# Reordered side tasks, a direct division and a split last projection in a two-layer attention kernel

## The chip, the cores and the metric

The kernel runs on one core of one Trainium2 chip, in one launch. The metric is the time of the device in microseconds. Before the change it was run three times: 3338.06, 3339.32 and 3341.99 us, median 3339.32. One execution more was profiled. Engines are named as in the profile: PE is TensorE (PEld its weight loads), ACT ScalarE, DVE VectorE, POOL GpSimd, SP the engine that issues most transfers.

## The reference

The input x has 4 images of 256 channels and 64 x 64 pixels, in float32. Two attention layers follow each other, each behind a group norm of 32 groups and with a residual:

```
x = x + L0(_gn(x))        # layer 0
x = x + L1(_gn(x))        # layer 1

L0: q = Wq x;  k, v = 2x2 convolutions of x with stride 2 (1024 positions)
    attn = softmax((q·k + q·(rel_h + rel_w)) * 32**-0.5) per head, 8 heads of 32
    out = v attn
L1: q, k, v = 1x1 convolutions (w_qkv, b_qkv)
    the 4096 pixels are cut into 4 areas of 1024; softmax attention within each area
    out = out + depthwise 7x7 convolution of v (w_pe, b_pe)
    out = 1x1 convolution (w_proj, b_proj)
```

The softmax is computed without subtracting the maximum; the kernel sums divisors and reciprocals into `sums` and checks at the end that none is out of bounds, for which a second path stands ready.

## The kernel before

**Units and steps.** The attention of both layers is cut into 128 units: 8 blocks (`BLOCKS`: layer 0, written A, of images 0 to 3, then layer 1, written B, of images 0 to 3) of 16 units. A unit is one half of the channels (4 heads) of one chunk of 512 queries against 1024 keys, and has 8 steps of 128 keys. So the main loop has 1024 steps. In step j TensorE computes four score matmuls into two PSUM pairs (`scores`, L262), ScalarE exponentiates each pair (`exps`, L266), TensorE multiplies the probabilities of the step before with v (`weighted`, L273), and VectorE adds the probabilities to those of step 0 (`sum_up`, L795: two additions of 128x1024 per step, except for the first step of a unit). When a unit's eight steps are done, its `av` is copied out (L816), and three steps after its last step, which is step 2 of the next unit, the summed probabilities are multiplied with ones (`divisors`, L282).

**Division.** `divide` (L291 to L312) copies the divisors, sends one row per head through DRAM to 128 partitions of 16 numbers, takes the reciprocals there (step 7 of the next unit), sends them back and spreads them, and multiplies in step 4 of the unit after that. The four transfers are issued by GpSimd. Only the last unit takes the reciprocal of the whole 128x512 tile on VectorE (L294) and multiplies at once; its divisors and reciprocals are kept in `spare` and summed later by `sum_last`, two reductions.

**Side tasks.** All other work (projections for q, k and v, the depthwise convolution as matmuls, the output projection) is cut into tasks of one to four parts. `plan` is a dictionary from (unit, step) to functions, filled by `plan_a`, `plan_b`, `plan_values` and `plan_conv`; `at(g, j, f)` enters one. A function either issues something at once (a transfer on SP, a normalization on ScalarE, statistics on VectorE) or appends a task to the queue `side`. After a step's attention the loop executes one part if the queue isn't empty, a second one if more than 7 parts wait and a third one if more than 14 wait, one less in step 2, and all of them of one task. `soon_tasks` inserts tasks directly behind the head instead of appending them. `need(made, key)` executes parts at once until what an attention step needs exists: q and k when a step's scores are issued, v when its first weighted product is issued (that is in step 1 of a unit, behind the scores of that step). `plan_conv` uses it too, for the last values. Every task's result goes into one PSUM tile, `side`, with one buffer, and is copied out by ScalarE or VectorE at the end of the task.

**Tasks by layer.** For layer 0 of image b, `plan_a` loads the image's chunks for the statistics (`look`, `add_stats`) from unit `early`, forms the norm, and for each of four areas loads two chunks, normalizes eight `taps` on ScalarE and appends two k and two v tasks. `prep` is the first unit of the block before. Queries (`make_q`) are appended two units ahead of their use. For layer 1, `plan_b` appends k, v and q tasks; `plan_values` computes the values that the convolution reads, `plan_conv` is the convolution (units 70.5 to 106), and after it come the projections (`add_conv` adds convolution, bias and attention, `project` multiplies and adds the residual): those of images 0 to 2 are spread over units 108 to 125, those of image 3 follow their own attention. All chunks share one tag with six buffers, the taps one with three, and the probabilities one with ten.

**The end.** The last chunk's projection starts when unit 127's attention has been multiplied: VectorE adds both halves of the channels, TensorE multiplies two tasks, VectorE adds bias and residual, and one transfer writes 512 KB. Then `sums` is compared with its limit, the count goes to a register, and the program ends.

The loop around all this:

```
ps[j], exps = scores(units[g], j)
exps[0]()
for f in later.pop(now[0], []): f()      # sums, divisors, divide
if before is not None: weighted(*before)
exps[1]()
do(g, j)                                  # the plan's functions
# then one to three parts of the queue's head
```

Of the kernel before, what the change touches and what calls it, by code (L numbers as in the profile page):

```python
# [12 lines left out]
ALU = mybir.AluOpType  # L13
AX = mybir.AxisListType

P = 128
# [38 lines left out]
def direct_path(  # L55
# [149 lines left out]
    def plan_norm(key, g, j):  # L205

        name = f"{key[0]}{key[1]}"
        made = {}

        def aggregate():  # L210
            for tag, cols in (("mv", 2), ("gmean", 1), ("dev", 1), ("gvar", 1)):
                shape = [P, CT, cols] if cols > 1 else [P, CT]
                made[tag] = pool.tile(shape, FP, tag=tag, name=f"{tag}_{name}", bufs=2)
            mv = made["mv"]
            for t in range(CT):
                V.bn_aggr(out=mv[:, t, :], in_=stats[key][:, t].rearrange("p c s -> p (c s)"))

        def means():
            mv, mean, dev = made["mv"], made["gmean"], made["dev"]
            ps = ps_pair(f"gm_{name}")[:, 0, :CT]  # L220
            T.matmul(ps, lhsT=gmat, rhs=mv[:, :, 0], start=True, stop=True)
            S.copy(mean, ps)
            V.tensor_sub(dev, mv[:, :, 0], mean)
            V.tensor_mul(dev, dev, dev)
            V.tensor_add(dev, dev, mv[:, :, 1])

        def variances():
            ps = ps_pair(f"gv_{name}")[:, 0, :CT]
            T.matmul(ps, lhsT=gmat, rhs=made["dev"], start=True, stop=True)
            S.activation(made["gvar"], ps, AF.Identity, bias=eps)  # L230
            norm = pool.tile([P, 2, CT], FP, tag="norm", name=f"norm_{name}", bufs=8)
            shift, rstd = norm[:, 0, :], norm[:, 1, :]
            G.tensor_tensor(rstd, made["gvar"], neghalf, ALU.pow)
            G.tensor_tensor(shift, made["gmean"], rstd, ALU.mult)
            G.tensor_scalar(shift, shift, -1.0, None, ALU.mult)
            norms[key] = shift, rstd

        at(g, j, aggregate)
        at(g, j + 1, means)
        at(g, j + 3, variances)  # L240

    def normalize(key, dst, src, t):
        shift, rstd = norms[key]
# [34 lines left out]
    def divisors(g, p):  # L278

        dens[g] = ps_pair("den")[:, 0, :]  # L280
        for h in range(4):
            T.matmul(  # L282
                dens[g][HD * h : HD * h + HD, :], lhsT=ones, rhs=p[h // 2][:, h % 2, :], start=True, stop=True,
            )

    def divide(g, unit):

        den_sb = pool.tile([P, CH], FP, tag="den", name="den_sb", bufs=1)
        few = pool.tile([P, 2, CH // HD], FP, tag="few", name="few", bufs=2)
        rows = dram.tile([4, CH], FP, tag="rows", name=f"rows_{g}", bufs=4)  # L290
        S.copy(den_sb, dens.pop(g))  # L291
        if g == len(units) - 1:
            rb = pool.tile([P, CH], FP, tag="p", name="rb", bufs=10)
            V.reciprocal(rb, den_sb)  # L294
            V.tensor_mul(unit[4]()[:, unit[0], :], avs.pop(g), rb)
            spare.extend((den_sb, rb))
            return
        G.dma_start(rows, den_sb[0:P:HD, :])  # L298
        G.dma_start(few[:, 0, :], rows.rearrange("h (q n) -> (h q) n", n=CH // HD))
# [23 lines left out]
    def plan_a(b, u, prep):  # L323

        key = ("A", b)

        early = prep - (5 if b else 0)
        areas = {}

        seen = {}  # L330
# [66 lines left out]
            at(early + c // 2, 4 * (c % 2) + 3, lambda c=c: add_stats(c))  # L397
        plan_norm(key, early + 4 if b != 1 else 0, 1)
        for a in range(NAREA):
            g = prep + (2 + 3.1 * a if b else 6 + 2.2 * a)  # L400
            at(0, int(NKT * (g - 1.6)), lambda a=a: load(a))
            for n in range(8):
                at(0, int(NKT * (g - 1.1)) + n, lambda a=a, n=n: make_taps(a, n))
            for n in range(2):
                at(0, int(NKT * (g + 0.6 * n)), lambda a=a, n=n: task(4, make_k, a, n))
                at(0, int(NKT * (g + 0.6 * n + 1.2)), lambda a=a, n=n: task(4, make_v, a, n))
# [58 lines left out]
    def plan_b(b, u):  # L465
# [76 lines left out]
            for half in range(2):  # L542
                at(g - 3, 2 + 5 * half, lambda a=a, half=half: load_v(a, half))
        for c in range(NCH):
            for qd in range(2):
                at(u + 2 * c - 2, 4, lambda c=c, qd=qd: task(2, make_q, c, qd))

        rest, made_x = {}, {}

# [15 lines left out]
                nc.sync.dma_start(att, attd[b][c])  # L565
            rest[c] = cv, att

        def add_conv(c):
            cv, att = rest[c]
            if c < NCH - 1:  # L570
                load_residual(c)
            if att is None:
                att = atts["B", b, c]
            for t in range(CT):
                V.scalar_tensor_tensor(cv[:, t, :], cv[:, t, :], bpe_sb[:, t : t + 1], att[:, t, :], ALU.add, ALU.add)

        def project(c, to):
# [9 lines left out]
            if to == 1:  # L587
                rest.pop(c)
                nc.sync.dma_start(ov[b][:, :, c * CH : (c + 1) * CH], made_x.pop(c))


        for c in range(NCH):
            g, j = u + 2 * c + 3, 5
            if b < B - 1:
                at(g, j + 1, lambda c=c: store_att(c))
                g, j = 0, int(NKT * (late + spread * (b * NCH + c)))
            else:
                at(g, j, lambda c=c: add_conv(c))
                at(g, j + 2, lambda c=c: soon_tasks([(2, project, c, to) for to in range(CT)]))
                g, j = (g - 1, 5) if c < NCH - 1 else (g - 2, 2)  # L600
# [46 lines left out]
    def plan_values(b, c, start):  # L647
# [794 lines left out]
```

## Time and profile before

| | |
|---|---|
| median of three runs | 3339.32 us |
| the profiled execution, its own time | 3342.12 us |
| its span | 3340.4 us |
| mean TensorE clock granted in it | 0.997 |
| first score matmul | 83.3 us after the span's start |
| last score matmul | 3306.8 us |
| `p<-p` additions on VectorE (L795) | 1792, 2117.9 us |
| exponentials on ScalarE (L266) | 2048, 2018.8 us |

Times inside the profile count from the span's start. A line of the page's groups gives engine, operation, output and input tiles, how many, the busy time and the mean of one. In a timeline the first two numbers are start and duration, and brackets give the idle time ahead of the instruction and what ended it. In a table of windows, each engine's busy time is followed by the number of its instructions; the last three columns are the granted clock, the share of the transfer engines and GB/s. On TensorE each float32 matmul has two records, so a step's scores are 8 records, its weighted products 8, and one part of a projection task 8.

### The profile page before, as it was taken

The numbers are of one execution on the slowest core, as the hardware profiler recorded it, in microseconds if no ns is written. First come the engines' busy times: TensorE is split into PE (matmuls) and PEld (weight loads), VectorE is DVE, ScalarE is ACT, GpSimd is POOL, SyncE is SP. The second block draws the span as 40 slices with busy tenths as digits, with TensorE's granted clock in tenths as the row PEclk, the third lists the DMA queues.
The fourth block names the chain that finished last, engine by engine and source line by source line (L and its number), as shares of the span: only waits on it lengthen the run. The fifth ranks groups of instructions, "written<-read, shape, count | busy, mean of one in ns | idle before, by whom it ended". The sixth has DMA issues, their size and how long they took to land.

```text
span 3340.4 us, 76594 instructions
## 1 busy us (share of the span) xinstructions
PE 3277.4 (98%) x31778; PEld 1019.4 (31%) x31778; DVE 2461.7 (74%) x2589; ACT 2560.4 (77%) x3057; POOL 490.3 (15%) x925
## 2 busy tenths in 40 slices
PE   7999999999999999999999999999999999999997
PEld 4233323332233322222223333333333332222221
DVE  3778997778877787777866666666666667778777
ACT  3888788888888888888887777777777777766665
POOL 0111112111211111111111111111111111111111
PEclk9999999999999999999999999999999999999999
DMA  4322221222322124543246565666656554445441
GB/s 175 78 65 69 93 84 55 95 95 79 98 82 79 52 65 131 154 125 114 90 121 151 144 167 141 150 151 153 163 130 164 143 143 136 153 150 174 147 135 62
DMA packets 307580, 397.52 MB, mean 119 GB/s; under 512 B 182652, under 2 KB 199324, under 8 KB 306904
## 3 DMA queue, kind: packets, MB, share of 16 engines
q1 hardware_dynamic: 278776, 356.06, 36.7%
q0 software_dynamic: 28448, 36.48, 4.3%
q8 instruction: 252, 4.13, 0.5%
q14 instruction: 104, 0.85, 0.1%
HBM read 285.98 MB, written 106.42 MB: 117 GB/s over the span
## 4 chain that ended last, share of the span: by engine, by line
PE 93%; ACT 2%; issue 2%; DVE 1%; DMA 1%; SPq 0%; POOL 0%; DVEq 0%; ACTq 0%; POOLq 0%
PE s L262 32%; PE av L273 28%; PE conv_ps L730 5%; PE den L282 4%; PE k0ps L156 3%; PE q1ps L156 3%; PE v0ps L156 3%; PE ops L156 3%; PE k1ps L156 3%; PE q0ps L156 3%; PE vals_ps L156 3%; PE v1ps L508 2%; ACT p L266 1%; DVE p L795 1%; DVE xm L586 0%
## 5 line engine op out<-in xcount | busy, mean ns | idle before, releaser
L795 DVE TENSOR_TENSOR p<-p 128x1024 f32<-128x1024 f32 x1792 | 2117.9, 1221 | 728.4 <-ACT p L266 649.5
L266 ACT ACTIVATE p<-s 128x1024 f32<-128x1024 f32 x2048 | 2018.8, 1027 | 569.3 <-PE s L262 561.8
L262 PE MATMUL s<-q,k_A 32*128 32x512 f32 x4096 | 606.7, 640 | 1.4 <-ACT p L266 0.9
L262 PE MATMUL s<-q,k_B 32*128 32x512 f32 x4096 | 588.5, 640 | 0.7 <-ACT p L266 0.4
L273 PE MATMUL av<-p,v_A 128*32 128x512 f32 x4096 | 551.7, 604 | 0.0
L273 PE MATMUL av<-p,v_B 128*32 128x512 f32 x4096 | 544.9, 603 | 0.0
L309 POOL DMA_DIRECT2D rb<-recs x508 | 252.9, 503 | 406.8 <-DMA recs<-few 347.0
L262 PEld LDWEIGHTS s<-q,k_A 32*128 32x128 f32 x4096 | 175.8, 183 | 354.5 <-issue 270.7
L307 POOL DMA_DIRECT2D recs<-few x127 | 70.3, 554 | 1412.3 <-DVE sums L306 1346.2
L262 PEld LDWEIGHTS s<-q,k_B 32*128 32x128 f32 x4096 | 162.3, 182 | 336.9 <-issue 275.2
L273 PEld LDWEIGHTS av<-p,v_A 128*32 128x32 f32 x4096 | 89.3, 108 | 382.7 <-issue 334.7
L273 PEld LDWEIGHTS av<-p,v_B 128*32 128x32 f32 x4096 | 88.6, 108 | 369.7 <-issue 332.9
L730 PE MATMUL conv_ps<-rows,band 126*32 126x256 f32 x3072 | 193.9, 380 | 0.0
L730 PEld LDWEIGHTS conv_ps<-rows,band 126*32 126x32 f32 x3072 | 125.0, 139 | 106.8 <-issue 69.6
L298 POOL DMA_DIRECT2D rows<-den_sb x127 | 74.8, 589 | 558.0 <-ACT den_sb L291 552.4
L156 PE MATMUL ops<-cv,wp_sb 128*32 128x512 f32 x1024 | 129.9, 606 | 15.1 <-DVE xm L586 8.1
L282 PE MATMUL den<-p,ones 128*32 128x512 f32 x1024 | 137.9, 605 | 0.4 <-DVE p L795 0.4
L156 PE MATMUL k0ps<-taps,wk_sb 128*32 128x256 f32 x2048 | 131.1, 384 | 3.0 <-ACT taps L244 3.0
L156 PE MATMUL vals_ps<-hv,wqkv_sb 128*32 128x512 f32 x1024 | 129.8, 596 | 2.7 <-ACT vout L672 2.7
L156 PE MATMUL q1ps<-h,wqkv_sb 128*32 128x512 f32 x1024 | 128.6, 592 | 2.6 <-DVE xm L586 2.6
L156 PE MATMUL k1ps<-h,wqkv_sb 128*32 128x512 f32 x1024 | 128.4, 593 | 2.2 <-DVE xm L586 1.4
L156 PE MATMUL q0ps<-hq,wq_sb 128*32 128x512 f32 x1024 | 129.8, 592 | 0.0
(91 smaller groups left out, 1720.9 us busy)
## 6 DMA issues: line engine op xcount, KB each, us to landing
rb<-recs POOLq DMA_DIRECT2D x508, 64.0 KB, 2.3
rows<-vals SPq DMA_DIRECT2D x128, 189.0 KB
rows<-vals SPq DMA_DIRECT2D x128, 188.8 KB
rows<-vals SPq DMA_DIRECT2D x128, 188.7 KB
valc<-vout SPq DMA_DIRECT2D x32, 576.0 KB
vals<-vout SPq DMA_DIRECT2D x256, 72.0 KB
vc<-valc SPq DMA_DIRECT2D x32, 576.0 KB
hq<-in_x SPq DMA_DIRECT2D x32, 512.0 KB
```

The lines of the kernel that those rows point to most:

```text
L156: T.matmul(out[cols, :], lhsT=lhsT[:, cols], rhs=rhs, start=start, stop=stop)
L262: T.matmul(pairs[h // 2][:, h % 2, :], lhsT=k[rows, unit[0], j * P : (j + 1) * P], rhs=q[rows, :], start=True, stop=True,)
L266: exps = [lambda i=i: S.activation(p[i], pairs[i], AF.Exp, scale=SCALE) for i in range(2)]
L273: T.matmul(av[HD * h : HD * h + HD, :], lhsT=v[:, j, unit[0] * P + HD * h : unit[0] * P + HD * h + HD], rhs=p[h // 2][:, h % 2, :], start= ...
L282: T.matmul(dens[g][HD * h : HD * h + HD, :], lhsT=ones, rhs=p[h // 2][:, h % 2, :], start=True, stop=True,)
L298: G.dma_start(rows, den_sb[0:P:HD, :])
L307: G.dma_start(recs.rearrange("h (q n) -> (h q) n", n=CH // HD), few[:, 1, :])
L309: G.dma_start(rb[HD * h : HD * h + HD, :], recs[h : h + 1, :].to_broadcast([HD, CH]))
L508: T.matmul(ps[HD * i : HD * i + HD, m, t * P : (t + 1) * P], lhsT=vcs[a, n // 2][:, t, 4 * (n % 2) + 2 * m + i // 2, HALO + HD * (i % 2) : ...
L730: T.matmul(ps[HD * m : HD * m + HD, i], lhsT=band_tiles[k][:, g, :, part + c], rhs=xs[:, m % 2, c, :, 3 * g : 3 * g + WW], start=(g == 0), ...
L795: soon(1, lambda i=i: V.tensor_add(ps[0][i], ps[0][i], ps[j][i]))
```

## The change

Six things are changed, all in the order of issue but for the division and the last projection:

- `plan_norm`: the group means are formed two steps behind the statistics instead of one, the variances four instead of three.
- `divide`: the last two units, instead of one, take the reciprocal of the whole tile. For unit 126 the two reductions of the check follow at once (`sum_den`) and the multiply is entered for step 6 of unit 127. `sum_last` goes; unit 127's reductions are issued by `project_last`.
- `plan_a`: the statistics of images 2 and 3 start one unit earlier; the areas' tasks start at 2 + 3.3a (image 1) and 0.3 + 3.8a (images 2, 3) units from `prep`, where they started at 2 + 3.1a.
- `plan_values`: the values of image 1 start 4.5 units earlier and are 1.2 units apart instead of 1.0; the tasks are appended one step later behind their load.
- `plan_b`: the query tasks of layer 1 are put directly behind the queue's head.
- The last chunk: the first half of its channels is added in step 7 of unit 127, the second when the attention is there; `project_last` multiplies the first half with both output halves, then the second, in one PSUM pair, and writes each output half with its own transfer.

```diff
-        at(g, j + 1, means)
-        at(g, j + 3, variances)
+        at(g, j + 2, means)
+        at(g, j + 4, variances)
...
+    def sum_den(g, *tiles):
+        for n in range(2):
+            V.tensor_reduce(sums[:, n, g : g + 1], tiles[n], AX.X, ALU.add)
...
-        if g == len(units) - 1:
+        if g >= len(units) - 2:
             rb = pool.tile([P, CH], FP, tag="p", name="rb", bufs=10)
             V.reciprocal(rb, den_sb)
-            V.tensor_mul(unit[4]()[:, unit[0], :], avs.pop(g), rb)
-            spare.extend((den_sb, rb))
+            mul = lambda: V.tensor_mul(unit[4]()[:, unit[0], :], avs.pop(g), rb)
+            if g == len(units) - 1:
+                mul()
+                spare.extend((den_sb, rb))
+            else:
+                sum_den(g, den_sb, rb)
+                at(g + 1, 6, mul)
             return
...
-        early = prep - (5 if b else 0)
+        early = prep - (0, 5, 6, 6)[b]
...
-            g = prep + (2 + 3.1 * a if b else 6 + 2.2 * a)
+            g = prep + (6 + 2.2 * a, 2 + 3.3 * a, 0.3 + 3.8 * a)[min(b, 2)]
...
-            for qd in range(2):
-                at(u + 2 * c - 2, 4, lambda c=c, qd=qd: task(2, make_q, c, qd))
+            at(u + 2 * c - 2, 4, lambda c=c: soon_tasks([(2, make_q, c, qd) for qd in range(2)]))
...
-        def add_conv(c):
+        def add_conv(c, ts=range(CT)):
...
+        def project_last(c):
+
+            cv, xm, ps = rest[c][0], made_x[c], ps_pair("ops")
+            add_conv(c, [1])
+            sum_den(len(units) - 1, *spare)
+            for t in range(CT):
+                for to in range(CT):
+                    product(
+                        ps[:, to, :], lhsT=wp_sb[:, t, to * P : (to + 1) * P], rhs=cv[:, t, :],
+                        start=(t == 0), stop=(t == CT - 1),
+                    )
+            for to in range(CT):
+                V.scalar_tensor_tensor(xm[:, to, :], ps[:, to, :], bproj_sb[:, to : to + 1], xm[:, to, :], ALU.add, ALU.add)
+                nc.sync.dma_start(ov[b][:, to, c * CH : (c + 1) * CH], xm[:, to, :])
...
+                if c == NCH - 1:
+                    at(g - 2, 7, lambda c=c: add_conv(c, [0]))
+                    at(g, j, lambda c=c: project_last(c))
+                    at(g - 2, 2, lambda c=c: load_rest(c))
+                    continue
...
-            at(0, when + 7, lambda t=t: task(2, values, t))
+            at(0, when + 8, lambda t=t: task(2, values, t))
...
-    def sum_last():
-        for n in range(2):
-            V.tensor_reduce(sums[:, n, len(units) - 1 :], spare[n], AX.X, ALU.add)
-
-    at(len(BLOCKS) * UNITS + 1, 6, sum_last)
...
-            plan_values(b, c, ends[b] + 1.8 + (14.5 if b == 1 else 0) + (3.4, 1.0, 1.6, 0.4)[b] * c)
+            plan_values(b, c, ends[b] + 1.8 + (10 if b == 1 else 0) + (3.4, 1.2, 1.6, 0.4)[b] * c)
```

More of the change, by code (lines that the diff above doesn't have):

```diff
@@ L573, in add_conv @@
                 att = atts["B", b, c]
-            for t in range(CT):
+            for t in ts:
                 V.scalar_tensor_tensor(cv[:, t, :], cv[:, t, :], bpe_sb[:, t : t + 1], att[:, t, :], ALU.add, ALU.add)
@@ L597, in plan_b @@
             else:
+                if c == NCH - 1:
[3 more added lines that the diff above has]
+                    continue
                 at(g, j, lambda c=c: add_conv(c))
                 at(g, j + 2, lambda c=c: soon_tasks([(2, project, c, to) for to in range(CT)]))
-                g, j = (g - 1, 5) if c < NCH - 1 else (g - 2, 2)
+                g, j = g - 1, 5
             at(g, j, lambda c=c: load_rest(c))
```

## The prediction

> **What bounds the kernel now.** First the head of the page.
>
> ```profile
> span 3340.4 us, 76594 instructions
> PE 3277.4 (98%) x31778; PEld 1019.4 (31%) x31778; DVE 2461.7 (74%) x2589; ACT 2560.4 (77%) x3057; POOL 490.3 (15%) x925
> PE 93%; ACT 2%; issue 2%; DVE 1%; DMA 1%; SPq 0%; POOL 0%; DVEq 0%; ACTq 0%; POOLq 0%
> ```
>
> TensorE is busy nearly throughout and carries 93% of the chain of waits. The amount of its work is fixed, and this change adds no matmul; so what can be won is time in which a modelled "busy" hides a wait. To find it I cut the main loop into its 128 units at the first score matmul of each and read the table of windows (unit 13, 15, 17, 47, 18, 50, 123), together with one line of the chain that gives the dense rate.
>
> ```profile
> 79.97 3.43 PE q0ps L156 x32
> ...
> 386.19:410.49 24.30, 24.30 (x268) 8.19 (x264) 21.58 (x25) 17.55 (x21) 3.70 (x7) 1.00 0.23 69
> 432.10:452.24 20.14, 20.14 (x144) 5.71 (x140) 17.27 (x23) 16.70 (x22) 6.19 (x10) 1.00 0.15 42
> 474.01:493.44 19.43, 19.43 (x141) 5.59 (x137) 15.54 (x15) 19.42 (x27) 3.15 (x6) 1.00 0.16 48
> 1201.90:1220.20 18.30, 18.30 (x140) 4.65 (x136) 14.83 (x14) 16.23 (x19) 3.15 (x6) 1.00 0.14 42
> 493.44:522.97 29.53, 28.30 (x272) 9.46 (x269) 23.23 (x30) 22.32 (x29) 6.76 (x11) 1.00 0.29 97
> 1264.00:1293.12 29.12, 27.58 (x203) 7.21 (x199) 20.87 (x29) 23.12 (x30) 7.02 (x11) 0.94 0.41 131
> 3181.81:3221.71 39.90, 35.59 (x348) 9.98 (x344) 27.19 (x33) 19.82 (x23) 6.24 (x12) 1.00 0.40 140
> ```
>
> 32 records in 3.43 us are 0.107 each, so half a projection task (8 records) is 0.857. The timeline of the last unit shows bare steps 2.06 and 2.24 us apart. A unit of eight bare steps with its divisors is 8 x 2.07 + 0.86 = 17.4; unit 13 with eight side parts should take 17.4 + 8 x 0.857 = 24.3, and takes 24.30: a filled unit has no loss. Unit 47, with nothing in the queue, loses 18.3 - 17.4 = 0.9, or 0.13 per empty step (step 2 holds the divisors and doesn't count); unit 17, whose empty steps also carry a normalization on ScalarE (x27 against x19), loses 2.0, or 0.29 each. Unit 18 (layer 1's norm) loses 3.1, unit 50 (norm, with a clock of 0.94) 5.3. Summed over units 0 to 59 the loss is 37 us of 1426. That is all that moving tasks about can address there. Then two places of another kind. In unit 123 the loss is 5:
>
> ```profile
> 3208.66 1.92 PE L156 MATMUL ops<-cv,wp_sb 128*32 128x512 f32 x16 [0.81 <-ACT q L530]
> ...
> 3211.46 1.92 PE L156 MATMUL ops<-cv,wp_sb 128*32 128x512 f32 x16 [0.88 <-DVE xm L586]
> 3213.45 0.75 DVE L586 SCALAR_TENSOR_TENSOR xm<-ops,bproj_sb,xm 128x512 f32<-128x512 f32 x1 [2.05 <-PE ops L156]
> ...
> 3221.85 0.69 ACT L530 ACTIVATE q<-q1ps,bqkv_sb 128x512 f32<-128x512 f32 x1 [13.24 <-PE q1ps L156]
> ```
>
> A call of `need` empties the queue at once. All tasks share one PSUM tile (`side`, one buffer), so every task waits about 0.85 for the copy of the one before, and no attention runs. Last the end:
>
> ```profile
> 3294.61 3.55 DVE L795 TENSOR_TENSOR p<-p 128x1024 f32<-128x1024 f32 x3 [0.89 <-ACT p L266]
> 3296.90 0.59 ACT L291 COPY den_sb<-den 128x512 f32<-128x512 f32 x1
> ...
> 3311.25 2.35 DVE L795 TENSOR_TENSOR p<-p 128x1024 f32<-128x1024 f32 x2
> 3315.38 3.35 DVE L294 RECIPROCAL rb<-den_sb 128x512 f32<-128x512 f32 x1 [1.11 <-ACT den_sb L291]
> 3320.75 1.41 DVE L575 SCALAR_TENSOR_TENSOR cv<-cv,bpe_sb,att_B 128x512 f32<-128x512 f32 x2
> 3321.60 6.55 PE L156 MATMUL ops<-cv,wp_sb 128*32 128x512 f32 x32 [6.04 <-issue]
> 3328.22 0.75 DVE L586 SCALAR_TENSOR_TENSOR xm<-ops,bproj_sb,xm 128x512 f32<-128x512 f32 x1 [2.17 <-PE ops L156]
> ```
>
> In the last unit VectorE, not TensorE, finishes last: its sums run to 3313.60 while the last `av` ends at 3310.45. Then comes a serial tail, and 11.4 us of program end after the last `xm` (3328.97 to 3340.4).
>
> [...] after 6 us of idling the last 32 records take 6.55 us, against 3.43 warm. [...]
>
> **Layer 0's tasks over their block, values of b=1 earlier.** Nothing is added or removed; taps, k, v and the statistics move. I walked the queue by its rule through units 0 to 59, counting the steps (but step 2) in which no part runs. Before: 70 (seven each in units 1, 15, 17, 31, 47; three each in 0, 14, 16, 46, 48, 49, 58, 59; nine more), 34 of them with a normalization on ScalarE. After: 59, 43 with one. Units 17, 33, 46, 47 and 49 are filled, units 8, 11, 23, 27, 35, 56 and 57 get holes, and the first taps of b=2 and 3 now fall in units 15 and 31, where the queue is still empty. By the prices above: before 34 x 0.29 + 36 x 0.13 = 14.5, after 43 x 0.29 + 16 x 0.13 = 14.6. So 0. Bounds -4 and +4: dense ScalarE steps (unit 52 loses 1.6, 42 0.9) thin out, but unit 35 packs about 22.5 us of ScalarE on 21.7 of TensorE, and unit 28 some 24.3 us of VectorE (sums 15.9, statistics 2.4, k's additions 4.8, the rest 1.2) on 23.4. The half clock in unit 50 costs about 1.5 (an `av` group took 1.71 for 1.06, a projection half 1.95 for 1.04); unit 49 is fuller now and it may not return: -0.9. Chunk loads on SP move with this. The most live chunks in layer 0 stay below six, so SP shouldn't block.
>
> **Norms one step later.** In unit 18 the group-mean matmul waits 1.23 for the statistics behind other DVE work; a step later it doesn't: -1.2. But the variances now share step 3 with the first `hv` normalization of b = 0, 2, 3, which stands right behind them on ScalarE, with the next exponentials queued behind it. It waits for GpSimd's three small operations (1.38, 0.52, 0.53 in unit 18); so far it waits 1.5 us there. I work out the new end from the same rows as 0.8, 1.0 and 0.4 later in units 18, 50, 66: +2.2. Together +1.0 (0 to +2). Layer 0's own norms keep their cost, about 1.8 (unit 15's loss of 2.7 less unit 47's 0.9), in units 14 and 30.
>
> **Layer 1's queries first.** `soon_tasks` puts them behind the head. In the convolution units the same parts run in another order, which are already at the floor: 0 (-1 to +2). At unit 70 `plan_conv` forces what stands ahead of the last values: three parts so far, with two waits (1.63); now two query tasks stand there as well, seven parts and four waits: +1.6. In units 112, 116, 120, 124 the walk says that the bursts don't vanish. With q done, k1 and v1 tasks have been pushed back, and `need` of v forces 6, 6, 6 and 9 parts in step 1, where 6, 7, 7 and 11 were forced in steps 0 and 1. Waits: before 2.1 + 3.9 + 3.1 + 5.0 = 14.1 (losses of units 112, 115, 119, 123). After, at 0.88 behind an `ops` task and 0.9 behind a `v1` task (0.25 until its copy starts at 3227.11 in the timeline, 0.59 for the copy, some 0.05): 112 has 0.2 + 0.88 + 0.88 + 0.9 = 2.9, 116 and 120 0.88 + 3 x 0.9 = 3.6 each, 124 0.2 + 3 x 0.88 + 2 x 0.9 = 4.6; sum 14.7. +0.6 (-3 to +3, since the v1 copies share ScalarE with step 1's exponentials).
>
> **The end.** Unit 126's division now runs on VectorE in step 2 of unit 127, ahead of that step's sums. VectorE is idle from 3293.7 (its sums of unit 126 are done) until den_sb at 3297.5; then reciprocal 3.4 and two reductions 1.25 to 3302.2; then seven pairs of sums at 2.27, the multiply of unit 125 (0.65), the add of c=6 (1.33), the multiply of unit 126 (0.65) and the half add (0.66): 19.2, to 3321.4, where 3313.6 was. Divisors, copy and the last reciprocal follow as before (1.78 and 3.35) to 3326.5. Multiply 0.65, xm 0.67, half add 0.7 to 3328.6. Of the last projection half is done; the other 16 records take 1.7 warm or 3.4 cold, with the reductions (1.25) beside them, and the last xm ends at 3331.3 (warm) or 3333.0 (cold), where it was 3328.97. +3.1 (+2 to +4.5). The output halves gain nothing: the program's end, not the output transfer, closes the span. What is saved (GpSimd's four transfers of unit 126) lay beside this.
>
> **Sum.** 0 - 0.9 + 1.0 + 1.6 + 0.6 + 3.1 = +5.4 on the profiled execution's 3342.1 (span 3340.4 and 1.7 around it), so 3347.5. That execution lies 2.8 above the median of the runs, 3339.3; on that scale 3344.7. A difference within 0.2% (6.7 us) can't be told from none, so my forecast is "no change, leaning slow".
>
> **Rivals.** (1) The smoothing works as meant. Units 14 to 18, 31 to 34 and 46 to 50 lose 25 us now; if two thirds of it went and nothing new came, -16 + 5 = -11 and 3328. For it: unit 13 shows that filled units lose nothing. Against it: the count of holes with ScalarE work in them. (2) Slower: the `chunk` slots. If slots are handed out in strict rotation, the third statistics load of b=2 takes the slot of the seventh `hq`, which the queue frees at unit 11, step 4, while its statistics stand on VectorE at step 3, with the sums behind them. VectorE would stand some 6 us, and the divisors in unit 12, step 2 would come 4.5 to 6 late: 3339.3 + 5.4 + 5.3 = 3350. It decides once the load lands more than a step late. Against it: the `p` tiles (ten buffers, two per step, the first pair held ten steps) could not work in rotation. (3) The last unit has slack that I miss, the tail gains the 4 us of the projection: 3339.3 + 2.3 - 4 = 3338.
>
> **Chances.** Forecast 0.62, rival 1 0.19, rival 2 0.13, rival 3 0.06. The forecast's own range is 3337 to 3352: of its 0.62 about 0.02 are faster, 0.37 same, 0.23 slower. Rival 1 gives 0.15 faster and 0.04 same, rival 2 0.13 slower, rival 3 0.06 same. Faster 0.17, same 0.47, slower 0.36. The range reaches to rivals on both sides: 3331 to 3353.
>
> **What would show it.** Windows: units 17, 33 and 47 near 23.4 to 25.2 us with no loss, 15 and 31 still about 20; unit 70 longer by 1.6 beyond its parts; four bursts of `v1ps` in step 1 of units 112, 116, 120, 124 with ScalarE copies as releasers. At the end two rows of the wide reciprocal, and the sums of unit 127 ending 31.4 us after its first score, where 23.7 was. I am wrong if units 14 to 50 shrink by more than 10 us in all, or if the last xm comes earlier, counted from the start of unit 127, than the 39.0 us of before.

## The result and the profile after

The changed kernel takes 3341.78 us (median of 6 runs, 3339.87 to 3342.75), the kernel before 3339.41 us (6 runs beside it). The ratio is 1.0006 with a 95% interval of 0.9993 to 1.0019: no difference that this measurement can tell from none. The profiled execution took 3341.92 us and the one of before 3342.12, so the two profiles agree more closely than the medians; why is told below.

The head of the page for the changed kernel, with the chain of waits by engine:

```profile
span 3340.1 us, 76533 instructions
...
PE 3275.8 (98%) x31778; PEld 1018.0 (30%) x31778; DVE 2463.9 (74%) x2590; ACT 2557.2 (77%) x3057; POOL 485.0 (15%) x918
...
PE 80%; ACT 2%; DVE 1%; issue 1%; DMA 0%; SPq 0%; POOL 0%; DVEq 0%; ACTq 0%; POOLq 0%
```

TensorE has the same 31778 records and is as busy as before; GpSimd has seven instructions less (unit 126's transfers, which four lines of the kernel issue), VectorE one more. The chain's shares add up to 84% only: it isn't followed over the whole span here, so the 80% aren't a drop from 93%.

The table of windows, units 13, 15, 17, 47, 18, 50, 70 and 124 of the changed kernel, from the first score matmul of each to that of the next:

```profile
383.80:407.30 23.50, 23.50 (x228) 7.17 (x224) 23.47 (x27) 17.65 (x21) 3.68 (x7) 1.00 0.21 61
431.60:451.10 19.50, 19.50 (x150) 5.50 (x146) 15.66 (x15) 18.56 (x26) 3.18 (x6) 1.00 0.16 46
475.00:498.50 23.50, 23.50 (x240) 7.18 (x236) 18.11 (x19) 18.02 (x21) 3.13 (x6) 1.00 0.26 86
1200.30:1223.70 23.40, 23.40 (x196) 5.83 (x192) 19.05 (x21) 19.15 (x23) 3.13 (x6) 1.00 0.41 121
498.50:525.70 27.20, 26.26 (x276) 8.46 (x272) 19.88 (x25) 20.45 (x27) 6.10 (x11) 1.00 0.18 66
...
1270.80:1298.40 27.60, 26.57 (x196) 7.65 (x192) 20.25 (x29) 22.66 (x30) 5.46 (x11) 1.00 0.32 94
1754.00:1789.30 35.30, 32.05 (x320) 9.12 (x316) 17.06 (x21) 22.55 (x27) 3.68 (x7) 1.00 0.55 155
...
3204.70:3240.40 35.70, 31.66 (x337) 9.52 (x332) 23.22 (x27) 19.72 (x24) 4.12 (x8) 1.00 0.35 116
```

Units 17 and 47, which were nearly empty (19.43 and 18.30 us), now hold tasks and last 23.4 to 23.5 us without loss, and 15 is still short, as announced. Unit 18 is 2.3 us shorter. Unit 50 shows a clock of 1.00 where it was 0.94. Units 70 and 124 show the bursts: TensorE busy is 3 to 4 us short of the window there.

The end, from VectorE's timeline (start, duration; in brackets the idle time before and what ended it). Unit 127 begins at 3285.63:

```profile
3293.21 3.35 DVE L298 RECIPROCAL rb<-den_sb 128x512 f32<-128x512 f32 x1 [3.80 <-ACT den_sb L295]
3296.48 0.63 DVE L288 TENSOR_REDUCE sums<-den_sb 128x1 f32<-128x512 f32 x1
3297.02 0.67 DVE L288 TENSOR_REDUCE sums<-rb 128x1 f32<-128x512 f32 x1
3297.61 6.89 DVE L818 TENSOR_TENSOR p<-p 128x1024 f32<-128x1024 f32 x6
...
3314.42 2.35 DVE L818 TENSOR_TENSOR p<-p 128x1024 f32<-128x1024 f32 x2
3316.69 0.74 DVE L594 SCALAR_TENSOR_TENSOR xm<-ops,bproj_sb,xm 128x512 f32<-128x512 f32 x1
3319.41 3.35 DVE L298 RECIPROCAL rb<-den_sb 128x512 f32<-128x512 f32 x1 [1.98 <-ACT den_sb L295]
...
3324.07 0.74 DVE L583 SCALAR_TENSOR_TENSOR cv<-cv,bpe_sb,att_B 128x512 f32<-128x512 f32 x1
...
3327.72 1.41 DVE L611 SCALAR_TENSOR_TENSOR xm<-ops,bproj_sb,xm 128x512 f32<-128x512 f32 x2 [1.72 <-PE ops L156]
```

The first wide reciprocal and its two reductions stand ahead of the sums, which end at 3316.77, 31.1 us after the unit's start (23.7 before). The last `xm` ends at 3329.1, 43.5 us after it (39.0 before). That 39.0 comes from an execution whose last projection ran at half clock (granted 0.50 from 3320.69 to 3327.51 us): in the six traces that have the same instructions in unit 127, the last `xm` ends 37.6 to 39.0 us after the start, so differences at the end are known from traces to 1.5 us only.

What the two profiles say together, with each unit's loss over its floor reckoned as in the prediction (in the v and convolution units the floor is rough by 0.4 us):

| | loss before, us | after, us |
|---|---|---|
| units 0 to 59 | 37.3 | 31.7 |
| of it unit 50, half clock in the one, none in the other | 5.3 | 4.5 |
| units 60 to 71 | 7.0 | 8.6 |
| units 72 to 107 | -4.3 | -3.7 |
| units 108 to 126 | 15.2 | 15.4 |
| unit 127's start to the last `xm` (a duration) | 39.0 | 43.5 |

About 5.6 us are won in units 0 to 59, about 2.4 given back in layer 1 and 4.5 at the end. One execution doesn't tell which of the six edits did which, so the parts were run one by one.

### The profile page after: what moved, and what is told of

It is laid out like the page before. It is cut to its first block, busy times and chain, and to the rows that moved or that the text cites. A ratio compares the mean times of both kernels' runs of the same rounds, so it can differ in the third digit from the quotient of the medians.

```text
span 3340.1 us, 76533 instructions
## 1 busy us (share of the span) xinstructions
PE 3275.8 (98%) x31778; PEld 1018.0 (30%) x31778; DVE 2463.9 (74%) x2590; ACT 2557.2 (77%) x3057; POOL 485.0 (15%) x918
## 3 DMA queue, kind: packets, MB, share of 16 engines
q8 instruction: 252, 4.13, 0.5%
## 4 chain that ended last, share of the span: by engine, by line
PE 80%; ACT 2%; DVE 1%; issue 1%; DMA 0%; SPq 0%; POOL 0%; DVEq 0%; ACTq 0%; POOLq 0%
PE s L262 27%; PE av L273 24%; PE conv_ps L758 5%; PE q1ps L156 3%; PE k1ps L156 3%; PE den L282 3%; PE vals_ps L156 3%; PE ops L156 3%; PE q0ps L156 2%; PE v1ps L517 2%; PE v0ps L156 2%; PE k0ps L156 1%; ACT p L266 1%; DVE p L818 1%; DVE xm L594 0%
## 5 line engine op out<-in xcount | busy, mean ns | idle before, releaser
L156 PE MATMUL v0ps<-wv_sb,taps 128*32 128x256 f32 x2048 | 127.3, 379 | 0.9 <-ACT v_A L400 0.9
```

Of the source, the lines that this page charges most:

```text
L156: T.matmul(out[cols, :], lhsT=lhsT[:, cols], rhs=rhs, start=start, stop=stop)
```

## The experiments

Four kernels hold one part of the change each, on the kernel before; eight more test the reasons. Medians are given beside those of the kernel before measured with them. Two executions of the same instructions agree in nearly every unit within 0.03 us, so a part's effect is read from the units that it touches; the exceptions are the program's first 83 us (within 3.4 us), unit 50 and the end (clock; within 1.7 and 1.5 us), and unit 66 (within 0.5 us).

**The norms alone.**

```diff
-        at(g, j + 1, means)
-        at(g, j + 3, variances)
+        at(g, j + 2, means)
+        at(g, j + 4, variances)
```

> The kernel before with the norms alone (means two steps behind the statistics, variances four). The prediction's theory: units 18 and 50 save about 1.2 us of waiting for the group means, but the hv normalizations of units 18, 50 and 66 wait longer for the variances (0.8, 1.0, 0.4); sum +1.0 us, units 50 and 66 longer than 29.1 (28.2 without the half clock) and 27.0 us. The theory formed on the trace of the changed kernel, whose units 18, 34, 50 and 66 lose 1.5, 1.4, 0.7 and 0.45 us less than before: the later variances cost TensorE nothing, and the step in which the means' matmul stood in front of the scores is what goes; sum -2 to -4 us, unit 66 at 26.6 or less, with no change of its tasks.

Measured: 3336.17 us (21 runs) against 3339.66, ratio 0.9990 (0.9983 to 0.9996). Units 18, 34 and 66 are 1.10, 1.14 and 0.45 us shorter, and unit 50 takes 26.84 us against the 27.48 of executions without the half clock; units 15, 16 and 32 give 0.35 back. So 3.0 us are gained, where the prediction had +1.0: its sign was wrong. (The 0.45 of unit 66 alone is no more than that unit's spread.) The kernel before, units 18, 34, 50 and 66, from TensorE's timeline: `gm_B` is the matmul that forms the group means, `gmean_B` ScalarE's copy of them.

```profile
497.08 0.35 PE L221 MATMUL gm_B<-mv_B,gmat 128*128 128x2 f32 x2 [1.23 <-DVE few L305]
884.85 0.35 PE L221 MATMUL gm_B<-mv_B,gmat 128*128 128x2 f32 x2 [0.71 <-DVE few L305]
1267.93 1.13 PE L262 MATMUL s<-q,k_A 32*128 32x512 f32 x4 [0.28 <-ACT gmean_B L222]
1654.93 1.13 PE L262 MATMUL s<-q,k_B 32*128 32x512 f32 x4 [0.26 <-ACT gmean_B L222]
```

With the norms moved, units 18 and 34:

```profile
497.07 0.39 PE L221 MATMUL gm_B<-mv_B,gmat 128*128 128x2 f32 x2
884.48 0.38 PE L221 MATMUL gm_B<-mv_B,gmat 128*128 128x2 f32 x2
```

In units 18 and 34 the matmul itself waited for the statistics, in units 50 and 66 the scores behind it waited for the copy. TensorE stood idle for 2.5 us in the four together, and a step later its matmuls wait for the means nowhere.

And who waited for the finished norm (`norm_B`), before and with the norms moved:

```profile
  ACT hv L244: 5.2, 3
```

```profile
  ACT hv L244: 5.8, 3
```

The `hv` normalizations wait 0.6 us longer for the norm, not the 2.2 that were forecast, and they wait on ScalarE. GpSimd's timeline shows one reason. Before, in unit 18, with two VectorE rows below:

```profile
507.20 1.38 POOL L233 TENSOR_TENSOR norm_B<-gvar_B,neghalf 128x2 f32<-128x2 f32 x1
508.66 0.52 POOL L234 TENSOR_TENSOR norm_B<-gmean_B,norm_B 128x2 f32<-128x2 f32 x1
509.28 0.53 POOL L235 TENSOR_SCALAR norm_B<-norm_B 128x2 f32<-128x2 f32 x1
...
506.77 2.36 DVE L795 TENSOR_TENSOR p<-p 128x1024 f32<-128x1024 f32 x2 [0.50 <-ACT p L266]
509.05 0.69 DVE L312 TENSOR_TENSOR att_A<-av_sb,rb 128x512 f32<-128x512 f32 x1
```

With the norms moved:

```profile
505.69 0.79 POOL L233 TENSOR_TENSOR norm_B<-gvar_B,neghalf 128x2 f32<-128x2 f32 x1
506.57 0.19 POOL L234 TENSOR_TENSOR norm_B<-gmean_B,norm_B 128x2 f32<-128x2 f32 x1
506.85 0.22 POOL L235 TENSOR_SCALAR norm_B<-norm_B 128x2 f32<-128x2 f32 x1
```

The three operations take 1.2 us in place of 2.4. In the first case VectorE adds probabilities or multiplies all along; in the second it is idle from 506.5 to 508.9. (In unit 50 the last two keep their 0.52 and 0.53 with the norms moved, so this isn't the whole account.) In the kernel before the operation at 508.66 ends at 509.18, just after the addition that ran when it started (509.13), and the one at 509.28 ends at 509.81, just after the multiply (509.74).

**The means alone.** The variances stay three steps behind.

```diff
-        at(g, j + 1, means)
+        at(g, j + 2, means)
```

> The kernel before with the group means two steps behind the statistics instead of one, and the variances where they were, three steps behind. Theory A, after the norms alone saved 1.10, 1.14 and 0.45 us in units 18, 34 and 66 and 0.65 in unit 50 (against its 27.5 us of the executions without a half clock): it is the means' matmul, which stands in front of the scores and waits behind VectorE, so means alone save 0.7 to 1.2 in units 18, 34 and 50, 2.5 us or more in all. Theory B: it is the variances, whose GpSimd operations then fall into a gap of VectorE (0.19 and 0.22 us for the last two where 0.52 and 0.53 were) and end the wait of the hv normalization earlier; then means alone save under 1 us in all.

Measured: 3336.37 us (13 runs) against 3339.61, ratio 0.9990 (0.9982 to 0.9999), as good as both edits. Units 18, 34, 50 and 66 save 0.79, 0.77, 0.40 (against 27.48) and 0.62, together 2.6 (the 2.5 of idle time above); TensorE's matmuls wait for the means nowhere here either, and `hv` waits 5.7. Theory A holds: it is the means' place. Of 3.0 us, moving the variances adds at most a few tenths.

**Layer 0 alone.**

```diff
-        early = prep - (5 if b else 0)
+        early = prep - (0, 5, 6, 6)[b]
-            g = prep + (2 + 3.1 * a if b else 6 + 2.2 * a)
+            g = prep + (6 + 2.2 * a, 2 + 3.3 * a, 0.3 + 3.8 * a)[min(b, 2)]
-            at(0, when + 7, lambda t=t: task(2, values, t))
+            at(0, when + 8, lambda t=t: task(2, values, t))
-(14.5 if b == 1 else 0) + (3.4, 1.0, 1.6, 0.4)
+(10 if b == 1 else 0) + (3.4, 1.2, 1.6, 0.4)
```

> The kernel before with layer 0's areas, statistics and values moved as in the change, and nothing else. The prediction's theory: holes with a normalization in them take the place of the holes that are filled, units 0 to 59 lose as much as before (37.3 us over their floor by the bare step and the parts), within 4. The rival, from the trace of the changed kernel: filling 17, 33, 46, 47 and 49 saves 6.5 us and the new holes in 8, 11, 16, 32, 35, 56 and 57 cost 5 or more, so that 1.5 to 3 us remain as a gain. The smoothing rival of the prediction would have 10 us or more. Unit 50 tells whether its clock of 0.94 stays.

Measured: 3338.99 us (13 runs) against 3339.66, ratio 0.9997 (0.9988 to 1.0005): no difference that can be told. In the trace units 0 to 59 lose 35.75 us where they lost 37.30, and unit 67 0.65 less: 2.2 in all, less than the measurement can confirm. The filled units 17, 33, 46, 47 and 49 save 5.2, units 15 and 31 1.1 each; units 8, 32, 35, 48, 50, 56 and 57 give 6.8 back. The exchange of holes that was counted is what took place. Its clearest row is unit 35 (window, as above), with 30 instructions of ScalarE and 22 us of its time in 23.4:

```profile
912.10:935.50 23.40, 23.40 (x180) 5.88 (x176) 18.30 (x20) 22.02 (x30) 3.19 (x6) 1.00 0.10 36
```

It loses 1.7, where it lost nothing. Unit 50 has the clock of 0.94 in this execution as well (29.3 us).

**Layer 1's queries alone.**

```diff
-            for qd in range(2):
-                at(u + 2 * c - 2, 4, lambda c=c, qd=qd: task(2, make_q, c, qd))
+            at(u + 2 * c - 2, 4, lambda c=c: soon_tasks([(2, make_q, c, qd) for qd in range(2)]))
```

> The kernel before with layer 1's queries directly behind the queue's head, and nothing else. The prediction's theory: unit 70 forces seven parts with four waits instead of three parts with two (+1.6 us of loss there), the convolution units stay as they are, and the four bursts move from units 112, 115, 119 and 123 into step 1 of units 112, 116, 120 and 124 with 14.7 us of loss where 14.1 was; sum +2.2. The rival (the queries' purpose): a burst shrinks, since q is no longer what need has to force, and units 108 to 126 lose 3 us or more less than the 15.2 of before.

Measured: 3343.55 us (21 runs) against 3339.66, ratio 1.0013 (1.0006 to 1.0020): 3.9 us slower, where 2.2 were expected. By the trace 3.6 of them arise in units 70 to 107 and 0.2 in the four bursts, whose losses are 2.8, 3.2, 3.1 and 4.8 (expected 2.9, 3.6, 3.6, 4.6). Unit 70's window before, and with the queries in front:

```profile
1761.80:1792.40 30.60, 28.97 (x292) 8.51 (x288) 16.80 (x19) 21.71 (x26) 3.70 (x7) 1.00 0.67 185
```

```profile
1759.60:1794.80 35.20, 31.96 (x316) 9.08 (x312) 16.82 (x19) 22.48 (x27) 3.68 (x7) 1.00 0.54 156
```

It holds three parts more (24 records, 2.57 us) and is 4.6 us longer: 2.0 of waiting, 1.6 expected. The term that was missing stands in the next unit, in TensorE's timeline of the same kernel:

```profile
1800.76 1.22 PE L729 MATMUL conv_ps<-rows,band 126*32 126x256 f32 x16 [0.84 <-DMA rows<-vals]
```

The queries no longer stand between unit 70's burst and the first convolution, so that comes four steps earlier after the burst, before its rows have landed: that step takes 4.13 us where such a step takes 2.94, 1.2 of loss. The rival (shorter bursts) falls.

**The end alone.** The division of unit 126 and the last projection as in the diff of the change.

> The kernel before with the direct division of unit 126 and the last projection by halves, and nothing else. The prediction's theory: the wide reciprocal and two reductions of unit 126 (4.65 us), a multiply and the half add stand in front of unit 127's sums on VectorE, which end about 31 us after the unit's first score matmul instead of 23.7; half a projection is won back; the last xm ends 42 to 43.5 us after that first score where it was 39.0. The rival (the end's purpose): VectorE has slack in unit 127 and the last xm ends at 35 to 38.

Measured: 3343.38 us (13 runs) against 3339.66, ratio 1.0010 (1.0001 to 1.0018), so slower by about 3.7. In the trace the sums end 31.1 us after unit 127's start and the last `xm` 41.8 us after it, 2.8 to 4.2 later than where the end isn't changed (37.6 to 39.0). The rival falls: VectorE has no slack in unit 127. The same instructions in the changed kernel ended at 43.5; the 1.7 between them is TensorE's clock. After a gap of 3.4 to 3.5 us the last 16 records take 1.93 here and 2.80 there, and the eight divisor records after a gap of 2.36 take some 2.1 here and 3.0 there; the granted clock is 1.00 from 3318 to 3330 us here, and 0.50 from 3315.53 to 3318.94 and from 3325.77 on there.

**The end with unit 126 by the narrow path.** Only the last unit is divided directly; unit 126's reciprocals come two steps earlier and its multiply behind the last sums. The edit, against the end of the change:

```diff
-        if g >= len(units) - 2:
+        if g == len(units) - 1:
...
-        at(g + 1, 7, reciprocals)
-        at(g + 2, 4, multiply)
+        late = g == len(units) - 2
+        at(g + 1, 5 if late else 7, reciprocals)
+        at(g + 2, 0 if late else 4, multiply)
...
-                    at(g - 2, 7, lambda c=c: add_conv(c, [0]))
+                    at(g - 1, 1, lambda c=c: add_conv(c, [0]))
```

> The kernel before with the last projection by halves, but unit 126 divided through the narrow path, its reciprocals two steps earlier (step 5 of unit 127) and its multiply and the first half add behind the last sums of unit 127, in the 1.1 us in which VectorE waits for the last divisors. Theory: of the changed end only the wide division of unit 126 costs (4.65 us on VectorE in front of the sums); without it the sums end 23.7 us after the unit's first score again and the last xm ends at 34 to 37 us, where it was 39.0 (and 41.8 with the end of the change). Rival: the projection by halves has its own cost, and it stays at 38 or more.

Measured: 3335.48 us (21 runs) against 3339.61, ratio 0.9989 (0.9983 to 0.9996). VectorE's timeline at the end, unit 127 beginning at 3289.1:

```profile
3305.85 6.89 DVE L815 TENSOR_TENSOR p<-p 128x1024 f32<-128x1024 f32 x6
3312.66 0.68 DVE L316 TENSOR_TENSOR att_B<-av_sb,rb 128x512 f32<-128x512 f32 x1
3313.26 0.74 DVE L591 SCALAR_TENSOR_TENSOR xm<-ops,bproj_sb,xm 128x512 f32<-128x512 f32 x1
3313.92 0.74 DVE L580 SCALAR_TENSOR_TENSOR cv<-cv,bpe_sb,att_B 128x512 f32<-128x512 f32 x1
3314.58 3.34 DVE L298 RECIPROCAL rb<-den_sb 128x512 f32<-128x512 f32 x1
...
3323.70 1.41 DVE L608 SCALAR_TENSOR_TENSOR xm<-ops,bproj_sb,xm 128x512 f32<-128x512 f32 x2 [2.54 <-PE ops L156]
```

The sums end 23.6 us after the start again, multiply and half add fill VectorE's wait for the last divisors, and the last `xm` ends at 36.0. Against the 37.6 to 39.0 of the unchanged end that is 1.5 to 3 us (this execution, whose last 16 records take 3.59 us where the end alone took 1.93, was the slowest of the 21), at the median 4.1. So the halves of the last projection, together with the earlier reciprocals and the two separate transfers that this run doesn't part from them, are worth some 2 to 4 us, and the wide division of unit 126 costs more than that: 5.8 us lie between 36.0 and the 41.8 of the end alone.

**Query and v tasks in front.** For image 3 of layer 1 these go behind the head and behind those put there before (`front_task`), and k is appended as before.

```diff
+        put = front_task if b == B - 1 else task
...
-                at(g - 2, 1 + 3 * n, lambda a=a, n=n: task(1, make_v, a, n))
+                at(g - 2, 1 + 3 * n, lambda a=a, n=n: put(1, make_v, a, n))
...
-                at(u + 2 * c - 2, 4, lambda c=c, qd=qd: task(2, make_q, c, qd))
+                at(u + 2 * c - 2, 4, lambda c=c, qd=qd: put(2, make_q, c, qd))
```

> The kernel before with the query and the v tasks of layer 1, image 3, directly behind the queue's head (in their own order), k appended as before. Theory: a burst is set by whichever of q, k and v stands last in the queue, so it only changes its kind: by a walk through the queue need then forces 3, 9, 8 and 12 parts for k in step 0 of units 112, 116, 120 and 124, and units 108 to 126 lose 13 to 17 us as before (15.2). Rival: two of three kinds in front shorten the bursts, and 5 us or more go.

Measured: 3363.84 us (5 runs) against 3339.61, ratio 1.0072 (1.0058 to 1.0085). The rival falls, and the size expected fell too: units 108 to 126 lose 38.6, units 115 and 123 alone 13.5 and 17.5. In step 0 a burst stands in front of the unit's scores. From VectorE's and TensorE's timelines, units 115 and 123:

```profile
2974.15 1.42 DVE L585 SCALAR_TENSOR_TENSOR cv<-cv,bpe_sb,at 128x512 f32<-128x512 f32 x2 [4.03 <-DMA at<-attd]
```

```profile
3218.71 1.93 PE L156 MATMUL ops<-cv,wp_sb 128*32 128x512 f32 x8 [4.98 <-DVE xm L596]
3230.91 3.60 PE L156 MATMUL ops<-cv,wp_sb 128*32 128x512 f32 x16 [2.82 <-DVE xm L596]
```

Projections are forced before their attention has been fetched, and their copies stand on VectorE behind it; the granted clock is 0.89 and 0.91 over the two units' windows, and in unit 123 eight records behind the gap of 4.98 us take 1.93 and 16 behind that of 2.82 take 3.60, where 16 behind a gap of 0.89 take 1.92.

**The rule of the queue.** One line, on the kernel before:

```diff
-        for n in range((waiting > 0) + (waiting > 7) + (waiting > 14) - (j == 2)):
+        two, three = (2, 6) if g >= 108 else (7, 14)
+        for n in range((waiting > 0) + (waiting > two) + (waiting > three) - (j == 2)):
```

> The kernel before with one line changed: from unit 108 on a second part is executed when more than 2 parts wait and a third when more than 6 do (7 and 14 before). By a walk through the queue nothing is then left for need to force in units 112 to 124. Theory: what the bursts cost is the wait of each task for the one PSUM tile of the task before, 14 us in all, and it goes when the parts lie beside attention steps: units 108 to 126 lose 15.2 now and 1 to 4 then, 3326 to 3329 us at the median. Rival: the same parts cost as much in the steps (ScalarE's and VectorE's copies delay the exponentials and sums), and less than 5 us go.

Measured: 3323.58 us (5 runs) against 3339.61, ratio 0.9954 (0.9940 to 0.9967), 16.0 us faster and better than expected. Units 115, 119 and 123, which took 35.5, 35.3 and 39.9 us:

```profile
2948.10:2974.10 26.00, 26.00 (x268) 7.93 (x264) 22.14 (x23) 20.24 (x23) 3.15 (x6) 1.00 0.36 113
3060.70:3088.50 27.80, 27.80 (x288) 8.49 (x284) 21.51 (x24) 21.27 (x24) 3.76 (x8) 1.00 0.35 118
3173.40:3201.10 27.70, 27.70 (x286) 8.43 (x283) 22.09 (x26) 19.89 (x24) 3.69 (x7) 1.00 0.51 167
```

TensorE is busy all through them, and units 108 to 126 take 510.4 us where they took 526.0. The parts are the same; only none is forced any more. That the bursts' loss is the wait for the one PSUM tile rests on the gaps of 0.8 to 0.9 us in them; a second tile, which would test that wait by itself, wasn't tried.

**Together.** First the norms, the rule from unit 108 and the end by the narrow path; then layer 0 as in the change added; then the rule from unit 66 on, which empties unit 70's burst too.

> Three parts together on the kernel before: the norms of the change (-3.3 us in units 18, 34, 50, 66), the rule with 2 and 6 from unit 108 (-16.0 us at the median alone), the end with unit 126 divided through the narrow path (-4.1 alone). They lie in different stages, so the theory expects their sum: 3339.6 - 3.3 - 16.0 - 4.1 = 3316 us. Rival: the shorter queue at the end leaves more empty steps and the parts overlap, 3319 or more.

> The same with layer 0's areas, statistics and values moved as in the change. Theory: these save 2.3 us of loss with the old norms; with the new norms unit 50 (4.5 us of loss in the changed kernel, 3.0 with the norms alone) gives 1.5 of it back, so 0.5 to 1.5 us less than the version without, 3315. Rival: no difference or a loss.

> The best version so far (norms, layer 0, the rule, unit 126 by the narrow path) with the rule from unit 66 instead of 108. Theory: the burst of three parts with two waits in unit 70 goes as well, its 1.7 us of loss with it, and the convolution units stay at their floor: 3317.1 - 1.5 = 3315.5. Rival: with the queue short in the convolution units there are empty steps again, or the convolution's rows come late, and the time stays at 3317 or rises.

Measured, each with 5 runs: 3318.27 against 3339.95 (ratio 0.9934, 0.9921 to 0.9948), 3317.07 against 3339.95 (0.9930, 0.9916 to 0.9944), and 3316.13 against 3338.65 (0.9934, 0.9920 to 0.9947). The first falls 2 us short of the sum of its parts; the main loop and the rule's stage have the parts' own numbers (units 108 to 126 at 510.4 us), so the sum of medians was too hopeful. The second and third can't be told from the first by their intervals. In the traces layer 0 saves 2.4 on top of the others, of which 1.5 are hidden by a half clock in unit 50 of that execution (granted 0.50 for 3.4 us); the wider rule takes 2.05 of loss out of unit 70 (30.6 us, now 26.0 with fewer parts) and returns 1.8 in units 67 to 109, mostly in empty steps. All three beat both kernels by 21 us or more.

**The changed kernel with the rule from unit 66.**

> The changed kernel, with a second part from unit 66 on when more than 2 parts wait and a third when more than 6 do. By a walk through the queue need then forces nothing any more, in unit 70 either. Theory: what the queries in front cost is the longer burst in unit 70 and its follow (3.9 us measured alone) and what keeps the other four bursts is that v stays behind them; with no bursts left the changed kernel loses what the kernel before with the rule lost (16.0) and these 3.9: 3341.8 - 16.0 - 3 = 3323 or less. Rival: the queries in front have another cost in the convolution units (the first convolution waits for its rows, 1.2 us in unit 71), and 3326 or more stay.

Measured: 3326.03 us (5 runs, 3322.95 to 3327.95) against 3338.65, ratio 0.9961 (0.9947 to 0.9974). By its number this is the rival's case, but the rival's place is empty: units 70 and 71 lose nothing any more (the convolution's rows are there in time), 72 to 107 as much as in the changed kernel within 0.3 us, 108 to 126 0.2. In that execution unit 50 had a half clock (granted 0.50 for 3.4 us; 1.8 us of loss) and the end took 44.6 us from unit 127's start. That explains some 3 us of one execution. Whether it explains the median isn't settled, but the record leans that way: the four runs from 3325.62 us up have a mean granted clock of 0.996, and the one with 0.998 took 3322.95, as the theory has it.

## Why the prediction held, and which of its steps failed

The forecast was no change, leaning slow, at 3344.7; the medians say no change, leaning slow, at 3341.8. Step by step, with the part's trace and the part's median:

| step | predicted, us | in the trace | median of the part alone |
|---|---|---|---|
| layer 0 and values | 0 (-4 to +4) | -2.2 | -0.7 |
| half clock of unit 50 | -0.9 | chance | |
| norms | +1.0 (0 to +2) | -3.0 | -3.5 |
| queries: unit 70 | +1.6 | +2.0 | |
| queries: convolution units | 0 (-1 to +2) | +1.6 | |
| queries: bursts | +0.6 (-3 to +3) | +0.2 | +3.9 in all |
| end, against the 39.0 of before | +3.1 (+2 to +4.5) | +2.8 alone, +4.5 in the changed kernel | +3.7 |
| sum | +5.4 | | +3.4 |

- **Norms: the step that failed.** The prediction set -1.2 for the means against +2.2 for the variances. The first was right for the unit it was read from (18: 1.23 of waiting, 1.10 saved), but the step costs TensorE 0.71 in unit 34, 0.28 in unit 50 and 0.26 in unit 66 too, and these were left out. The second didn't come: the `hv` normalizations wait 0.6 us longer, and moving the variances changes the sum by tenths at most. Its price took the durations of GpSimd's small operations (1.38, 0.52, 0.53) along to another place, where in unit 18 they took 0.79, 0.19 and 0.22. "Together +1.0 (0 to +2)" was measured at -3.0 to -3.5, outside its bounds on the other side.
- **The half clock.** "Unit 49 is fuller now and it may not return" argued from a cause that doesn't decide. Executions whose instructions are the same up to there show unit 50 at 27.5 us (clock 1.00) and at 29.1 (0.94). It isn't the change's, and since the profiled execution of before had it, with an end up to 1.5 us longer than in other traces, and that of after hadn't, the two profiles agree better (3342.1 and 3341.9) than the medians (3339.4 and 3341.8).
- **Layer 0.** Right within its bounds: holes filled and holes made nearly cancel. (The 70 empty steps counted before are 68 by the prediction's own list, which changes the sum by 0.6 at most.) The rival that the smoothing works as meant falls; units 14 to 59 lose 7 us less in the changed kernel, the half clock and the norms included, not 16.
- **Queries.** The count of seven forced parts and the bursts that stay, only moved to step 1, were right, the bursts within 0.5 us each. Missing was what comes after a burst: the first convolution, drawn forward onto its own load (1.2 us). The bound of +2 held it.
- **End.** The sums' end was predicted 31.4 us after the unit's start and was 31.1; the last `xm` was predicted 41.4 (warm) to 43.1 us (cold) after it and came at 41.8 and 43.5. Rival 3 (slack at the end) falls with it. What was not seen is that the half projection and the direct division can be had apart, and that the first is a gain.
- **Rotation of chunk slots** (rival 2): unit 12 takes the same time in both kernels, so no VectorE stall of 6 us stands there. It falls.

So the near-zero result is a sum: by the traces about 5 us are won in layer 0 and the norms and about 7 given back by the queries and the end; 2.4 more than before are left at the median. Two of the prediction's terms were too high (the norms by 4, layer 0 by 2) and one too low (the queries by 1.7), so the forecast lay 3 us above the measured median and inside its range. That it landed there is in part luck: the term with the wrong sign was partly made up for by one that was too small, and a range of 15 us leaves room for both. What the experiments confirm in the main is the account of the queries and the end, not that of the norms.

What all of it had in common is that it moves tasks within a queue whose rule makes the bursts. Predicted for those was a cost that stays at 14 us wherever it falls; that the rule itself can remove it, for 16 us, is what the runs add.

## What to carry to other kernels

Where work is forced at the moment of need, putting one kind of task in front only changes which kind is late; serve the queue faster while attention steps still cover the tasks, and nothing is left to force. When an instruction is moved, look up its wait in every place where it runs, not in one; charge a wait that the move adds only if it holds up the engine that bounds the stage; and ask what the move draws forward onto a load that hasn't landed. An enabling edit (here the direct division, for the half projection) can cost more than what it enables: look for a cheaper one.

## What the runs showed of the hardware

- GpSimd's two small operations on 128x2 tiles (L234 and L235) stand 32 times in the traces of the two kernels. The ten that start while no VectorE instruction runs take 0.19 to 0.23 us. The 22 that start while one runs, always an addition `p<-p` or a multiply `att`, end 0.05 to 0.08 us after it; so they last 0.52 and 0.53 us in unit 18 and up to 1.07 us elsewhere.
- The half clock did not go with the length of a gap alone. In the last unit the changed kernel fell to half clock around gaps of 2.50 and 2.36 us; the end alone, with the same instructions there, fell around the first but kept full clock around gaps of 2.36 and 3.54. In the traces of the two kernels a stretch of half clock lasts 3.413 or 6.827 us (but for the last stretch, which the end of the profile cuts), and from one start to the next it is a whole number of steps of 3.413 us: 601 and 3 steps in the kernel before (1269.28 us in unit 50, 3320.69, 3330.93), 2 and 3 in the changed one (3308.70, 3315.53, 3325.77). Two such steps around the gap of 2.36 us, in the changed kernel and in the end alone (the clock stands third from the end):

```profile
3312.12:3315.53 3.41, 1.31 (x12) 0.13 (x4) 3.41 (x4) 0.00 (x0) 0.00 (x0) 1.00 0.00 0
3315.53:3318.94 3.41, 3.16 (x14) 1.20 (x18) 1.90 (x3) 0.14 (x1) 0.00 (x0) 0.50 0.02 5
```

```profile
3315.95:3319.37 3.42, 1.46 (x16) 0.25 (x8) 3.42 (x4) 0.00 (x0) 0.00 (x0) 1.00 0.01 2
3319.37:3322.78 3.41, 3.01 (x24) 0.85 (x28) 2.30 (x4) 0.59 (x1) 0.00 (x0) 1.00 0.02 5
```

After a step with 1.31 us of TensorE's work the clock is halved, after one with 1.46 it isn't; the gap of 3.54 is spread over two steps with 1.66 and 1.63. In the traces of the two kernels, from the first score matmul on and outside unit 50, five full-clock steps have at most 1.31 us of work (0.00 and 0.83 before, 0.91, 1.31 and 0.90 after), and half clock follows each of them; it follows none of the full-clock steps with more, of which the lowest reads 1.49. In unit 50 half clock comes in some executions and not in others (a clock of 0.94 over the unit, or 1.00), and after steps that read 3.04 us of work in the kernel before and about 1.9 in the changed kernel with the rule from unit 66; what brings it there isn't shown.
